# Strips added by transfers, unused matmuls and late loads of modes in an attention and spectral-convolution kernel

## The chip, the cores and the metric

The kernel runs on one core of a Trainium2 chip. The metric is the time of one launch on the device, in microseconds (us). A core has a matrix engine (TensorE, PE in the profile, with PEld for the loading of its stationary operand), VectorE (DVE), ScalarE (ACT), GpSimd (POOL) and SyncE (SP). Each engine works through its own instructions in order and waits on semaphores for what other engines produce. Transfers (DMA) are issued from the queues of SP, ACT and POOL and are carried out by 16 DMA engines. Matmul results land in PSUM, which has eight banks of 512 float32 columns for each of 128 partitions; everything else on the chip is in SBUF. TensorE does not always run at its full clock: the profile lists the clock that was granted to it, as a share of full speed.

## The reference

Four images of 64 channels and 96 x 96 pixels go through two layers with a residual each. The first is self-attention with a sigmoid in place of a softmax, followed by a gate for each channel; the second is a convolution that is done on 16 x 32 modes of a two-dimensional Fourier transform.

```python
def _L0_conv_ref(x, wq, bq, wk, bk, wv, bv, ca_w1, ca_w2):
    ...
    energy = jnp.einsum('bcn,bcm->bnm', Q, K)
    att = jax.nn.sigmoid(energy)
    out = jnp.einsum('bcm,bnm->bcn', V, att).reshape(B, C, H, W)
    out = out + x
    avg = out.mean(axis=(2, 3))
    mx = out.max(axis=(2, 3))
    ...
    scale = jax.nn.sigmoid(mlp(avg) + mlp(mx))
    return out * scale[:, :, None, None]

def _L1_conv_ref(u, W_pos_re, W_pos_im, W_neg_re, W_neg_im):
    ...
    u_hat = jnp.fft.rfft2(u, norm='ortho')
    top = jnp.einsum('bchw,cohw->bohw', u_hat[:, :, :k_h, :k_w], R_pos)
    bot = jnp.einsum('bchw,cohw->bohw', u_hat[:, :, H - k_h:, :k_w], R_neg)
    ...
    return jnp.fft.irfft2(v_hat, s=(H, W), norm='ortho')

x = x + _L0_conv_ref(_gn(x), ...)
x = x + _L1_conv_ref(_gn(x), ...)
```

`_gn` subtracts the mean and divides by the standard deviation of groups of two channels.

## The kernel before

The four images are two pairs; a pair's 2 x 64 channels fill the 128 partitions, and its 9216 pixels are the columns. A pair's pixels are cut into 18 blocks of 512 columns for the attention, and into 12 strips of 768 columns (eight rows of pixels, `STRIP`) for the second layer.

**Opening.** The first pair's nine pieces of 1024 columns come in through the queues of SP and ACT (L100). For each block VectorE takes statistics (`bn_stats`, L516) as it arrives, and beside it TensorE does a matmul whose result nobody reads (`warm`, L551 to L555, 256 columns, into bank 7; loop at L557 to L561, for the first 15 blocks). A 512-column one (L563) comes after the last step of the statistics. Small matmuls (L134, L142) average over groups; then the blocks are normalised (L151), and keys (L418), first queries (L459) and values (L429) are projected, with more `warm` matmuls between them.

**Attention.** For each block of 512 queries and each chunk of 128 keys TensorE does the energies (L474), ScalarE the sigmoid (L485), and TensorE the values times it (L503), which sums up in bank 0 or 7. This runs for both pairs, 36 blocks in all, in an order that the program lays out in lists (`mid`, `end`). While the second pair's attention runs, the second layer of the first pair is done in small steps between it (`Hidden`), its transfers all on SP's queue.

**Between attention and second layer, second pair.** After the last block `after(1)` (L525 to L549) takes mean and maximum over the pixels, does two small matmuls (L539, L544), and a sigmoid on ScalarE gives `gate`. `mv` is the mean after the gate (L762); a small matmul (L134) averages it over groups.

**Strips of the second pair.** Each strip becomes gate times the attention's result plus the image's original values, which were loaded again into the space of `vT` (called `again`, L688). For the strips named in `ADDED` ScalarE multiplies (L773) and a transfer issued by POOL adds (`accum_op`, L774); for the others VectorE does both in one instruction (`combine`, L164). Then VectorE transposes the strip in blocks of 32 (L781), ScalarE squares it for the variance (L782), and TensorE does three matmuls of the transform along the image's rows (L789) into `pa`. There are four strips to one `pa`; when they are done VectorE transposes it (`a`, L799), and two pairs of matmuls (`along_h`, L801) add to `pu`. The transposed strips rotate through four places (`t0` to `t3`). A scheduler that knows durations puts each engine's instructions in order; `tc.issue_after(x)` holds what is in it behind the instruction x.

**Modes and the way back.** With mean and rstd (L145 on POOL, L175) known, `pu` is scaled to `u` (L837 to L844). For eight groups of four mode rows, q = 0 to 7, `mix` (L192) multiplies with the weights (L205), two halves each, copied out of PSUM by VectorE and ScalarE in turn (L118, L120) into `vms[q]`. The weights of 32 rows come by transfers of 512 KB on POOL's queue: 9 during the attention (L680), 6 before the strips, 9 into `vT` once squares no longer need it (L821), and 8 into places of the strips (L733). The modes are turned by a round trip through DRAM: `vms[q]` is stored to `vd` (L217 whole, in turns on SP and POOL, for q up to 6; in four pieces of 64 KB, L221, for q = 7), and `vt` is loaded from it (L235, four loads of 64 KB for each half of the rows): the first half when q = 5 has been stored, on POOL's queue; the second when q = 7 has, on SP's and ACT's. TensorE then transforms back along height (`pz`, L868) and width (`py`, L887), VectorE adds to x1 (L889), and 24 transfers store the result (L892).

`occupy(n, behind, pool)` (L747 to L753) puts n unused matmuls of 512 columns behind a given instruction into a bank of its own: four behind the rstd's matmuls, ten behind the last of `mix`, two behind the last of `pz`.

Of the kernel before, what the change touches and what calls it, by code (L numbers as in the profile page):

```python
# [40 lines left out]
P = 128  # L41
B, C, H, W = 4, 64, 96, 96
# [3 lines left out]
R = C // 16  # L46
KW = 16
KH = 32
NB = 512
NBLK = N // NB  # L50
NCH = N // P
# [7 lines left out]
SIDE = 4  # L59
# [3 lines left out]
SQ = 32  # L63
NSQ = H // SQ
NSTRIP = N // STRIP
ADDED = (3, 6, 9)
GN_EPS = 1e-5


# [13 lines left out]
def tile_kernel(ctx: ExitStack, tc: tile.TileContext, x, cst, late, spec, out):  # L83
    nc = tc.nc
# [8 lines left out]
    cs = const.tile([P, NCONST], F32, tag="cs", name="cs")  # L93
    xs = []
    for p in range(NPAIR):
        xt = xpool.tile([P, N], F32, tag=f"x{p}", name=f"x{p}")
        for s in range(9):
            cols = bass.ts(s, N // 9)
# [7 lines left out]
    vT = xpool.tile([P, NCH, P], F32, tag="vT", name="vT")  # L106

    def named(name, rows=P):
        return cs[:rows, PLACE[name]]
# [43 lines left out]
    class Layer1:  # L153
# [38 lines left out]
        def mix(self, q, half):  # L192

            pv = self.bank(f"pv_{self.p}_{q}_{half}")  # L200
            for k in range(2):
                kw = half * 2 + k
                for g in range(4):
                    at = ((4 * q + g) * KW + SIDE * kw) * 4
                    self.last = nc.tensor.matmul(  # L205
                        pv[bass.ts(g, 32), :].rearrange("q (n k o) -> q n k o", n=SIDE, o=C)[
                            :, :, k, :],
                        self.ut[:, at:at + 32],
                        self.wts[4 * q + g].rearrange("q (n k o) -> q n k o", n=SIDE, o=C)[
                            :, :, kw, :], start=True, stop=True)  # L210
            vm = self.vms[q].rearrange("q (n m) -> q n m", n=SIDE)
            self.move(vm[:, :, bass.ts(half, 2 * C)], pv.rearrange("q (n m) -> q n m", n=SIDE))
            if half == 0:
                return

            if q < KH // 4 - 1 and self.p == 1:
                self.queues[q % 2].dma_start(  # L217
                    self.vd[4 * q:4 * q + 4].rearrange("h s m -> (h s) m"), self.vms[q])
            else:
                for g in range(4):  # L220
                    self.queues[g % 3].dma_start(self.vd[4 * q + g, :4 * SIDE],  # L221
                                                 self.vms[q][32 * g:32 * g + 4 * SIDE, :])

            if q in (5, 7):
                if self.vt is None:
                    self.vt = self.place_of_vt()
                row, M = 32 * KW * C, KW // SIDE * C
                first = KH // 2 * (q == 7)
                for b in range(2):
                    for slot in range(2):  # L230
                        to = 64 * b + 32 * slot + first
                        of = self.vd[first, 2 * slot + b, :]
                        of = bass.AP(tensor=of.tensor, offset=of.offset,
                                     ap=[[row, 16], [4 * KW * C + M, SIDE], [1, M]])
                        self.queues[1 if q == 5 else 2 * slot].dma_start(  # L235
                            self.vt[to:to + 16, :].rearrange("h (n m) -> h n m", n=SIDE), of)

    class Hidden(Layer1):

# [135 lines left out]
    with tc.tile_pool(name="work", bufs=1) as work, \  # L375
# [6 lines left out]
        banks = ps_s.tile([P, 8, NB], F32, tag="banks", name="banks")  # L382
        spare = [0]

        at = attp.tile([P, 14, NB], F32, tag="at", name="at")
# [13 lines left out]
            return u, h  # L399

        projected = [None]
        mark = [None]

        def low_or_high(dst, u, h, is_low):
# [72 lines left out]
        def place(i):  # L477

            t = burst[i]
            return 7 * (t % 2 + 1) - sizes[t] + i - total[t - 1]  # L480
# [16 lines left out]
        def attend(items):  # L497
            for pair, cols in items:
                n, j = divmod(pair, NCH)
                acc = banks[:, 7 - n % 2 * 7, :]  # L500
                for b in range(2):
                    half = slice(b * C, (b + 1) * C)
                    nc.tensor.matmul(acc[half, cols], vT[:, j, half], at[:, place(2 * pair + b), cols],  # L503
                                     start=(j == 0), stop=(j == NCH - 1))
                if j == NCH - 1 and cols.stop == NB:
                    p, m = divmod(n, NBLK)
                    blk = xs[p][:, bass.ts(m, NB)]
                    nc.vector.scalar_tensor_tensor(blk, acc, 1.0, blk, ALU.mult, ALU.add,  # L508
                                                   accum_out=sums[p][:, m:m + 1])
                    mark[0] = nc.vector.tensor_reduce(maxs[p][:, m:m + 1], blk, AX.X, ALU.max)  # L510
# [14 lines left out]
        def after(p):  # L525

            f = small.tile([P, 2], F32, tag="f", name=f"f_{p}")
            hid = small.tile([2 * R, 2], F32, tag="hid", name=f"hid_{p}")
            gate = small.tile([P, 1], F32, tag="gate", name=f"gate_{p}")

            def means():
                tot = small.tile([P, 1], F32, tag="tot", name=f"tot_{p}")
                nc.vector.tensor_reduce(tot, sums[p], AX.X, ALU.add)
                nc.vector.tensor_scalar(f[:, 0:1], tot, 1.0 / N, None, ALU.mult)
                nc.vector.tensor_reduce(f[:, 1:2], maxs[p], AX.X, ALU.max)

            def hidden():
                ph = bank_a(f"ph_{p}")
                nc.tensor.matmul(ph[:2 * R, 0:2], named("w1"), f, start=True, stop=True)  # L539
                nc.vector.tensor_scalar(hid, ph[:2 * R, 0:2], 0.0, None, ALU.max)  # L540

            def gates():
                pg = bank_a(f"pg_{p}")
                nc.tensor.matmul(pg[:, 0:2], named("w2", 2 * R), hid, start=True, stop=True)  # L544
                gsum = small.tile([P, 1], F32, tag="gsum", name=f"gsum_{p}")
                nc.vector.tensor_reduce(gsum, pg[:, 0:2], AX.X, ALU.add)
                nc.scalar.activation(gate, gsum, AF.Sigmoid)

            return gate, [means, hidden, gates], f  # L549
# [7 lines left out]
        each, norm0, _ = stats_of(0)  # L557
        for s, step in enumerate(each):
            last = step()
            if s < NBLK - 3:  # L560
                warm(s, NB // 2)  # L561
        with tc.issue_after(last.ins):
            warm(NBLK - 3)  # L563
# [9 lines left out]
        q = first_queries()  # L573
# [58 lines left out]
        first = begins[NBLK]  # L632
# [64 lines left out]
        for t in range(T):  # L697
# [15 lines left out]
            for step in end[t]:  # L713
                step()
        gate, steps, f = after(1)
        for step in steps:
            step()


    with tc.tile_pool(name="tail", bufs=1, reuse_waits="tile") as tail, \  # L720
# [26 lines left out]
        def occupy(n, behind, pool):  # L747


            pd = pool.tile([P, NB], F32, tag="idle", name=f"idle_{behind.ins.name}")  # L750
            with tc.issue_after(behind.ins):
                for _ in range(n):
                    nc.tensor.matmul(pd, cs[:, :P], cs[:, :NB], start=True, stop=True)  # L753
# [2 lines left out]
        l1 = Layer1(1, gate, lambda name: small_bank.tile([P, NB], F32, tag="m", name=name),  # L756
                    evacuate, (nc.sync, nc.gpsimd, nc.scalar))
        l1.wts = wts
        x1 = xs[1]

        mr, steps, mv = group_stats(None, l1.bank, "l1_1")
# [92 lines left out]
        for q in range(KH // 4):  # L854
            l1.mix(q, 0)
            l1.mix(q, 1)
        occupy(10, l1.last, mix_bank)


        banks.close()  # L860
# [118 lines left out]
```

## Time and profile before

| | |
|---|---|
| median of three runs | 3089.66 us (3088.97 to 3090.65) |
| the profiled execution | 3088.47 us |
| span in it, first to last instruction | 3086.7 us |
| TensorE busy | 3062.3 us (99%) |
| ScalarE busy | 2423.9 us (79%) |
| VectorE busy | 387.6 us (13%) |
| mean granted clock of TensorE | 0.996 |
| last attention matmul ends | about 2998.9 us |
| strips, from the gate to the last `pu` matmul | 3002.0 to 3031.5 us |
| mixing (L205) | 3036.24 to 3050.3 us |
| `pz` starts | 3059.29 us |

A row of a timeline or of the groups gives start or busy time, the engine, the line of the code, the operation, the tile written and the tiles read, and shapes and number. In brackets behind a row stands how long the engine had been idle before it, and what released it. A row of a stretch gives its ends and length, the busy time (and number of instructions) of PE, PEld, DVE, ACT and POOL in it, the granted clock, the mean busy share of the 16 DMA engines, and GB/s. The chain is followed backwards from the last instruction, at each step to what released it. Outside the three regions named in the table (opening, strips, way back) TensorE is occupied by the attention without a gap that matters.

### The profile page before, as it was taken

To read this page: it belongs to the slowest core of one execution; us is meant where nothing else is said; L and a number is where in the kernel's file an instruction comes from. 1 tells how busy PE (TensorE), PEld (TensorE's weight loads), DVE (VectorE), ACT (ScalarE), POOL (GpSimd) and SP (SyncE) were. 2 spreads that over 40 slices of the span, in tenths; PEclk is the share of its full clock that TensorE was granted. 3 is DMA by queue.
4 is the path that set the end of the run, shared out by engine and by line. 5 is a ranking of instruction groups with operands and counts; after the bars stand their busy time and mean duration, and the time that the engine had idled before them with its cause. 6 is when DMAs were issued, how large, how long until landed. Compare 5 with 4: busy or idle time off the path is not lost.

```text
span 3086.7 us, 42551 instructions
## 1 busy us (share of the span) xinstructions
PE 3062.3 (99%) x18910; PEld 1136.5 (37%) x18910; DVE 387.6 (13%) x818; ACT 2423.9 (79%) x1586; POOL 27.1 (1%) x52
## 2 busy tenths in 40 slices
PE   8999999999999999999999999999999999999998
PEld 4333333333333333334433333333333333333336
DVE  5200000000000000002312101010011000000015
ACT  4788888888888888887788887777777888888871
POOL 0000000000000000000000000000000100000001
PEclk9999999999999999999999999999999999999998
DMA  3000000000000000000134120322101300000026
GB/s 144 1 1 1 1 1 1 1 1 1 1 1 1 1 1 1 1 1 1 33 73 96 44 79 21 127 72 39 34 31 42 121 1 1 1 1 1 6 69 239
DMA packets 80488, 99.46 MB, mean 32 GB/s; under 512 B 48208, under 2 KB 58192, under 8 KB 80208
## 3 DMA queue, kind: packets, MB, share of 16 engines
q1 hardware_dynamic: 72032, 71.64, 8.2%
q0 software_dynamic: 5776, 20.45, 1.9%
q10 hardware_dynamic: 2496, 4.65, 0.4%
q8 instruction: 148, 2.42, 0.3%
q14 instruction: 36, 0.29, 0.0%
HBM read 67.49 MB, written 28.05 MB: 31 GB/s over the span
## 4 chain that ended last, share of the span: by engine, by line
PE 98%; DVE 1%; DMA 1%; issue 0%; SPq 0%; ACT 0%; ACTq 0%; DVEq 0%
PE banks L503 75%; PE banks L474 17%; PE banks L429 1%; PE banks L442 1%; PE banks L367 1%; PE banks L418 1%; PE banks L205 1%; PE py L887 0%; PE pv L205 0%; DMA x<-in_x_dram 0%; PE pa L789 0%; PE banks L345 0%; DVE x L164 0%; PE pu L801 0%; PE banks L293 0%; DVE xt L781 0%
## 5 line engine op out<-in xcount | busy, mean ns | idle before, releaser
L485 ACT ACTIVATE at<-banks 128x1536 f32<-128x1536 f32 (+1 forms) x1546 | 2401.4, 1599 | 589.8 <-PE banks L474 536.3
L503 PE MATMUL banks<-at,vT 128*64 128x512 f32 (+1 forms) x11728 | 2394.5, 549 | 0.0
L503 PEld LDWEIGHTS banks<-at,vT 128*64 128x64 f32 x11728 | 780.4, 136 | 1356.2 <-issue 1301.4
L474 PE MATMUL banks<-q,kT 32*128 32x512 f32 x5040 | 550.2, 453 | 0.0
L474 PEld LDWEIGHTS banks<-q,kT 32*128 32x128 f32 x5040 | 223.8, 182 | 455.9 <-issue 303.3
L508 DVE SCALAR_TENSOR_TENSOR x<-banks,x 128x512 f32<-128x512 f32 x36 | 24.9, 691 | 965.2 <-PE banks L503 965.2
L397 DVE TENSOR_SCALAR full_q<-banks,cs 128x256 f32<-128x256 f32 x35 | 16.9, 484 | 957.8 <-PE banks L442 957.8
L429 PE MATMUL banks<-cs,x 128*64 128x128 f32 x576 | 39.8, 279 | 0.7 <-DVE at L461 0.4
L452 DVE CAST q<-q 32x256 fp32r<-32x256 f32 x140 | 39.8, 284 | 3.8
L370 DVE TENSOR_TENSOR x<-banks,x 128x384 f32<-128x384 f32 x24 | 13.4, 557 | 197.0 <-PE banks L367 197.0
L429 PEld LDWEIGHTS banks<-cs,x 128*64 128x64 f32 x576 | 30.9, 136 | 14.6 <-DVE full_k L397 13.5
L406 DVE SCALAR_TENSOR_TENSOR q<-high_q,cs,full_q 64x256 fp32r<-64x256 f32 x70 | 33.6, 480 | 2.4
L397 DVE TENSOR_SCALAR full_k<-banks,cs 128x256 f32<-128x256 f32 x36 | 17.4, 484 | 92.0 <-PE banks L418 92.0
L636 DVE COPY ws<-banks 128x512 f32<-128x512 f32 x16 | 11.1, 691 | 134.6 <-PE banks L205 114.4
L433 DVE TENSOR_TENSOR vT<-banks,cs 128x512 f32<-128x512 f32 x36 | 24.8, 688 | 7.5 <-PE banks L429 7.4
L510 DVE TENSOR_REDUCE maxs<-x 128x1 f32<-128x512 f32 x36 | 24.7, 686 | 1.2
L418 PE MATMUL banks<-x,cs 128*64 128x256 f32 x144 | 23.7, 389 | 0.2 <-DVE full_q L397 0.2
L516 DVE BATCH_NORM_STATS2 stats<-x 128x6 f32<-128x512 f32 x36 | 22.2, 681 | 5.7 <-DMA x<-in_x_dram 5.4
L442 PE MATMUL banks<-x,cs 128*64 128x256 f32 x140 | 22.7, 403 | 0.0
L789 PE MATMUL pa<-xt,lc 128*128 128x256 f32 x72 | 18.9, 419 | 3.5 <-DVE xt L781 3.5
L367 PE MATMUL banks<-cs,ws 128*64 128x384 f32 x96 | 20.8, 512 | 0.0
L554 PE MATMUL banks<-x 128*128 128x256 f32 (+1 forms) x40 | 13.6, 484 | 6.0 <-DMA x<-in_x_dram 6.0
(129 smaller groups left out, 458.0 us busy)
## 6 DMA issues: line engine op xcount, KB each, us to landing
ws<-in_spec_dram SPq DMA_DIRECT2D x20, 512.0 KB
x<-in_x_dram SPq DMA_DIRECT2D x14, 512.0 KB
room<-in_spec_dram SPq DMA_DIRECT2D x12, 512.0 KB
w<-in_spec_dram POOLq DMA_DIRECT2D x10, 512.0 KB, 7.8
old<-in_x_dram SPq DMA_DIRECT2D x12, 384.0 KB
x1d<-x SPq DMA_DIRECT2D x12, 384.0 KB
xd<-old SPq DMA_DIRECT2D x12, 384.0 KB
xT<-xd SPq DMA_DIRECT2D x36, 128.0 KB
```

Of the source, the lines that this page charges most:

```text
L205: self.last = nc.tensor.matmul(pv[bass.ts(g, 32), :].rearrange("q (n k o) -> q n k o", n=SIDE, o=C)[:, :, k, :], self.ut[:, at:at + 32], s ...
L367: nc.tensor.matmul(py[bass.ts(b, C), :4 * W], self.z[:, i, bass.ts(b, C)], named("gw"), start=True, stop=True)
L397: nc.vector.tensor_scalar(u, src, bias, None, ALU.add)
L406: mark[0] = nc.vector.scalar_tensor_tensor(dst, h.bitcast(F32), is_low, u, ALU.mult, ALU.add)
L418: projected[0] = nc.tensor.matmul(pp[cols, :NB // 2], named("wk")[:, cols], src[:, e, :, :], start=True, stop=True)
L429: projected[0] = nc.tensor.matmul(pp[bass.ts(e, P // 2), bass.ts(i, P)], xs[p][:, bass.ts(2 * (4 * s + i) + e, P // 2)], named("wv"), star ...
L442: projected[0] = nc.tensor.matmul(pq[rows, :half], named("wq")[:, rows], xs[p][:, n * NB + e * half:n * NB + (e + 1) * half], start=True, ...
L452: nc.vector.tensor_copy(q[to:to + 32, cols], q[of:of + 32, cols])
L474: nc.tensor.matmul(banks[:, bank_of(t) + i - starts[t], :], kT[r:r + 32, i // 4, :], q[r:r + 32, :], start=True, stop=True)
L485: nc.scalar.activation(at[:, of + lo:of + hi, :], banks[:, bank + lo:bank + hi, :], AF.Sigmoid)
L503: nc.tensor.matmul(acc[half, cols], vT[:, j, half], at[:, place(2 * pair + b), cols], start=(j == 0), stop=(j == NCH - 1))
L508: nc.vector.scalar_tensor_tensor(blk, acc, 1.0, blk, ALU.mult, ALU.add, accum_out=sums[p][:, m:m + 1])
```

## The change

It has four parts.

- Opening: the loop that puts an unused 256-column matmul beside the statistics of a block does so for all 18 blocks.
- Between the values and the gate: an unused matmul of 512 and one of 256 columns, into bank 3, are put behind the last attention matmul, and four of 512 columns (`occupy`) behind the second small matmul of the gate. To name these two places, `attended` and `projected` now remember the instructions.
- Strips: `ADDED`, counted from 0, is 6, 8 and 10 in place of 3, 6 and 9.
- End: the loads of `vt` become a function of their own, `back`. For the first pair they stay where they were. For the second, the first half's loads come behind the last store of q = 7, followed by the second half's. The four last stores go to the queues of SP, ACT, ACT and POOL (pieces 0, 2, 3, 1) in place of SP, POOL, ACT, SP (pieces 0, 1, 2, 3). The number of unused matmuls behind the mixing is nine, not ten.

```diff
-ADDED = (3, 6, 9)
+ADDED = (6, 8, 10)
...
-                for g in range(4):
-                    self.queues[g % 3].dma_start(self.vd[4 * q + g, :4 * SIDE],
-                                                 self.vms[q][32 * g:32 * g + 4 * SIDE, :])
-
-            if q in (5, 7):
-                if self.vt is None:
-                    self.vt = self.place_of_vt()
-                row, M = 32 * KW * C, KW // SIDE * C
-                first = KH // 2 * (q == 7)
-                for b in range(2):
...
+                for g in (0, 2, 3, 1):
+                    stored = self.queues[min(g, 2)].dma_start(
+                        self.vd[4 * q + g, :4 * SIDE], self.vms[q][32 * g:32 * g + 4 * SIDE, :])
+
+
+            if self.p == 0 and q in (5, 7):
+                self.back(q)
+            elif q == 7:
+                with tc.issue_after(stored.ins):
+                    self.back(5)
+                self.back(7)
+
+        def back(self, q):
+            if self.vt is None:
+                self.vt = self.place_of_vt()
+            row, M = 32 * KW * C, KW // SIDE * C
+            first = KH // 2 * (q == 7)
+            for b in range(2):
+                for slot in range(2):
+                    to = 64 * b + 32 * slot + first
+                    of = self.vd[first, 2 * slot + b, :]
+                    of = bass.AP(tensor=of.tensor, offset=of.offset,
+                                 ap=[[row, 16], [4 * KW * C + M, SIDE], [1, M]])
+                    self.queues[1 if q == 5 else 2 * slot].dma_start(
+                        self.vt[to:to + 16, :].rearrange("h (n m) -> h n m", n=SIDE), of)
...
+        attended = [None]
...
-                    nc.tensor.matmul(acc[half, cols], vT[:, j, half], at[:, place(2 * pair + b), cols],
-                                     start=(j == 0), stop=(j == NCH - 1))
+                    attended[0] = nc.tensor.matmul(
+                        acc[half, cols], vT[:, j, half], at[:, place(2 * pair + b), cols],
+                        start=(j == 0), stop=(j == NCH - 1))
...
-                nc.tensor.matmul(pg[:, 0:2], named("w2", 2 * R), hid, start=True, stop=True)
+                projected[0] = nc.tensor.matmul(pg[:, 0:2], named("w2", 2 * R), hid,
+                                                start=True, stop=True)
...
-            if s < NBLK - 3:
+            if s < NBLK:
                 warm(s, NB // 2)
...
         gate, steps, f = after(1)
+        with tc.issue_after(attended[0].ins):
+            for n in (NB, NB // 2):
+                nc.tensor.matmul(banks[:, 3, :n], cs[:, :P], cs[:, :n], start=True, stop=True)
...
         l1.wts = wts
+        occupy(4, projected[0], small_bank)
...
-        occupy(10, l1.last, mix_bank)
+        occupy(9, l1.last, mix_bank)
```

More of the change, by code (lines that the diff above doesn't have):

```diff
@@ L219, in mix @@
             else:
-                for g in range(4):
-                    self.queues[g % 3].dma_start(self.vd[4 * q + g, :4 * SIDE],
-                                                 self.vms[q][32 * g:32 * g + 4 * SIDE, :])
-            if q in (5, 7):
-                if self.vt is None:
-                    self.vt = self.place_of_vt()
-                row, M = 32 * KW * C, KW // SIDE * C
-                first = KH // 2 * (q == 7)
-                for b in range(2):
[L230 to L236, printed above, removed]
+                for g in (0, 2, 3, 1):
[20 more added lines that the diff above has]
+                        self.vt[to:to + 16, :].rearrange("h (n m) -> h n m", n=SIDE), of)
     class Hidden(Layer1):
```

## The prediction

> **What bounds the kernel now.** I read the page first: its parts 1 and 4 say which engine sets the end, and the row of clocks in part 2 says where that engine is slowed.
>
> ```profile
> span 3086.7 us, 42551 instructions
> ...
> PEclk9999999999999999999999999999999999999998
> ...
> PE 98%; DVE 1%; DMA 1%; issue 0%; SPq 0%; ACT 0%; ACTq 0%; DVEq 0%
> ```
>
> TensorE carries 98% of the chain, and the attention (L503, L474) is 92% of it. None of the edits adds or removes an instruction between about 40 us and 2999 us, so some 2960 us stay as they are, and the case is about the first 30 us and the last 90. I therefore asked for the chain in order of time there, for the timeline of TensorE and VectorE, and for busy time and clock in short stretches. The chain of the last 90 us (start, us, what):
>
> ```profile
> 3013.95 2.70 DVE xt L781 x3
> 3016.65 0.04 issue
> 3016.69 1.56 PE pa L789 x6
> 3018.26 1.92 PE pu L801 x8
> 3020.17 5.38 PE pa L789 x24
> ...
> 3029.47 2.01 PE pu L801 x8
> ...
> 3051.36 4.45 DMA vd<-vm
> ...
> 3055.90 3.15 DMA vt<-vd
> 3059.05 0.25 issue
> 3059.29 4.61 PE pz L868 x32
> ```
>
> The reader is to see two hand-overs: VectorE holds the strips up to 3016.65 us and TensorE, never idle again, from there to 3031.48; and at the end two transfers in a row, stores of the modes (vd) and loads of them turned (vt), hold everything for 8 us. The same stretches with the clock that TensorE was granted (the number before the last two):
>
> ```profile
> 15.58:18.99 3.41, 0.80 (x5) 0.71 (x6) 2.36 (x6) 0.00 (x0) 0.00 (x0) 1.00 1.02 407
> 18.99:22.40 3.41, 3.41 (x8) 1.00 (x8) 1.70 (x5) 0.00 (x0) 0.56 (x1) 0.50 1.03 411
> ...
> 2998.82:3002.23 3.41, 0.63 (x6) 0.39 (x4) 2.19 (x11) 0.41 (x2) 0.00 (x0) 1.00 0.44 115
> 3002.23:3005.64 3.41, 1.09 (x3) 1.00 (x4) 3.41 (x6) 3.41 (x6) 2.38 (x3) 0.50 0.31 58
> 3005.64:3009.05 3.41, 3.41 (x9) 2.70 (x8) 3.41 (x5) 2.76 (x6) 1.41 (x3) 0.50 1.04 186
> ```
>
> A stretch in which TensorE did 0.6 to 0.8 us of work is followed by one at half clock, once after the statistics and once after the attention.
>
> **What the Trainium skill says.** "TensorE: Matmul & The Clock Gate", Part 1: The HAM clock gate, says that the clock halves after an idle window of about 3.4 us, comes back after a busy one, and that the windows run free of the kernel. This trace agrees: half clock lasts 18.99 to 22.40 (3.41 us) and 3002.23 to 3009.03 (6.80 us, two windows). So before, the place of the slow stretch differs from run to run. "DMA: Bandwidth & Descriptors", Issuing engines are not separate DMA queues, says that transfers issued by different engines share the same 16 DMA engines and interleave; that bears on the last edit, and the stretch 3051 to 3054.5 (DMA share 1.00, below) agrees.
>
> **The change, part by part.** Times are in the profiled execution, 3088.47 us long with a span of 3086.7; the median of the three runs is 3089.66.
>
> *Opening.* The unused matmuls on x run for all 18 blocks, not 15: three more of 256 columns. Six records took 1.56 us at 13.12, so TensorE works until about 16.24 rather than 14.68, and the statistics matmul comes at 17.49: no delay. The idle time between 14.68 and the 512-column filler at 18.82 (two tiny matmuls aside) is 4.1 us, longer than a window; it becomes 2.6. If the clock then stays full, the filler of 1.91 us takes 0.86 and the first keys no longer wait for it: block 0 is normalised by 20.37, keys take about 0.5 instead of 1.05 (to 21.0), their bias on VectorE 0.48 (to 21.5), the first query matmul 0.87 (to 22.4), and its bias starts at 22.5 instead of 23.63. That is 1.1 us, on the chain. A window placed so that it covers the remaining gap can still halve the clock; if work of under some 30% of a window halves it (23% did, at 15.58), a window must start within about 1.2 us of each 3.41 for that, one run in three, and in before within 2.8, four in five: an estimate. The difference of medians is then about half a step to one step: 0 to 1.1, taken as 0.65.
>
> *Between values and gate.* A filler of 512 and one of 256 columns are put behind the last attention matmul, four of 512 behind the gate's. By the four fillers at 3031.69 (0.86 us each at full clock) the first two take 1.3 us, 2998.9 to 3000.2; the gate's first matmul comes at 3000.74: free. The other four must wait for the sum of the gate, at 3001.75, and take 3.44: until 3005.25. The mean's matmul (L134), queued behind them, ends at 3005.55; its reader on VectorE comes only at 3021. The first strip's matmuls then start at 3005.55 instead of 3005.11, a loss of 0.45, but at full clock: strip 0 ends at 6.9 rather than 7.8. Is that worth anything? In before TensorE waits anyway at strip 3 until 3014.98, behind VectorE. I stepped both queues by the measured durations (combine 0.93, transpose 0.90, transpose of a 1.19, three strip matmuls 1.345, a pu pair 0.95) in the two programs' instruction orders. For before this gives 3031.2 (measured 3031.48); before with the fillers alone 3031.2 again. Alone they are worth 0; cover: VectorE.
>
> *Strips.* Strips 6, 8 and 10 are scaled on ScalarE and added by a transfer, instead of 3, 6 and 9; as many as before, so no work is added. What moves is VectorE's order:
>
> ```profile
> 3007.66 0.97 DVE L781 STREAM_TRANSPOSE xt<-x 128x768 f32<-128x768 f32 x1
> ...
> 3012.13 1.90 DVE L164 SCALAR_TENSOR_TENSOR x<-x,gate,vT 128x768 f32<-128x768 f32 x2
> 3013.95 2.69 DVE L781 STREAM_TRANSPOSE xt<-x 128x768 f32<-128x768 f32 x3
> 3016.57 1.25 DVE L799 STREAM_TRANSPOSE a<-pa 128x1024 f32<-128x1024 f32 x1
> ```
>
> The three transposes at 3013.95 are strips 3, 8 and 6: strip 3 stands behind the combines of 4, 5, 7, 8 and 10, so the first quarter's transpose (a, at 3016.57) and all its matmuls come late. After, strip 3 is combined and transposed with strip 2, by 3009.6, and a_0 follows strip 4 at 3012.3. Stepped in the same way, TensorE ends the strips at 3029.3 instead of 3031.2: 1.9 us. What is late next is TensorE itself, busy from 3012.4 with waits of under 0.1 us. The added strips landed in before 4.0 to 7.5 us after issue, so by about 3012.4; they are wanted at 3014.4, 3016.2 and 3020.8: hidden. Half clock up to 3009 would cost the new order only 0.1, up to 3011 1.1: here the fillers insure. POOL's queue also moves: five weight loads stand behind the rstd step on it rather than three before and two behind. Their issues stay near 3028 to 3031 while the mixing starts 1.9 us earlier. Rows 24 and later are used some 10.3 us into the mixing, at 3044.7, and landed 4.9 to 9.2 us after issue: hidden, about 4 us to spare.
>
> *End.* On the second pair of images the first half of the vt loads (four on POOL) goes behind the last stores, the last stores are SP one, ACT two, POOL one rather than SP two, ACT one, POOL one, and nine fillers follow instead of ten.
>
> ```profile
> 3048.39 0.54 POOL L235 DMA_DIRECT2D vt<-vd  x1 [3.57 <-PE pv L205]
> 3048.92 0.54 POOL L217 DMA_DIRECT2D vd<-vm  x1
> 3049.45 1.55 POOL L235 DMA_DIRECT2D vt<-vd  x3
> 3051.24 0.51 POOL L221 DMA_DIRECT2D vd<-vm  x1 [0.23 <-ACT vm L120]
> ```
>
> The store of vm 5 waited behind a load for 3048.39, though ScalarE had finished its half at 3047.5. And the DMA engines stood still just then:
>
> ```profile
> 3048.00:3049.50 1.50, 1.50 (x36) 1.09 (x32) 0.48 (x1) 0.58 (x1) 1.11 (x3) 1.00 0.05 14
> ...
> 3051.00:3054.50 3.50, 3.50 (x9) 1.52 (x8) 0.00 (x0) 0.00 (x0) 0.51 (x2) 1.00 1.00 307
> ...
> 3055.00:3057.00 2.00, 2.00 (x6) 0.95 (x5) 0.00 (x0) 0.00 (x0) 0.00 (x0) 1.00 0.02 3
> ```
>
> After, that store goes out 1.4 us earlier into the idle stretch, and 256 KB of loads leave the queue ahead of the last stores; these should be down near 3054 instead of 3055.8. The POOL loads are issued from 3051.75 to 3053.9 and flow while the stores' completion is awaited; with the 4.7 us median of such loads the last lands at 3058.6 at worst, with the 2.3 minimum at 3056.2. The last four loads (3.15 us) then end near 3057. Nine fillers of 0.86 end at 3058.2 where ten ended at 3059.05, so TensorE's fillers, not the loads, become what pz waits for: 0.9 us saved, bounds 0 and 1.1. If the loads are late, pz starts with them and the saving shrinks.
>
> Sum: 0.65 + 0 + 1.9 + 0.9 = 3.45 us. From the median, 3089.66 − 3.45 = 3086.2. From the profiled execution, which had its half clock, 3088.47 − (1.1 + 1.9 + 0.9) = 3084.6; three runs of before spread over 1.7 us, so I keep both in the range.
>
> **Rivals.**
> (a) Only the strips pay: the opening keeps its half clock by the phase of the windows and pz waits for POOL's late loads. 3089.66 − 1.9 = 3087.8. For it: the loads' spread of 2.3 to 5.1 us; against: idle DMA engines.
> (b) Slower: POOL's loads behind the last stores. Place: the four vt loads. Transfers issued on POOL took up to 9.2 us when the engines were full; the last, issued at 3053.9, would land at 3063.1, 4.0 us after 3059.05. Against 0.65 + 1.9 gained: 3091.1. It decides once the last load takes more than about 7.7 us. Against it: only 512 KB is in flight then.
> (c) Nothing moves: VectorE's total work for the strips is unchanged, and TensorE's too, so the order gives nothing: 3089.6. Against it: TensorE idles 3.5 us before strip matmuls.
> (d) More than the sum: every part at its upper bound and the wandering windows gone: 3083 or less.
>
> **How the numbers follow.** Forecast 0.60, (a) 0.24, (b) 0.08, (c) 0.04, (d) 0.04. What a measurement of this kernel can tell from no change is about 0.2%, 6.2 us. Forecast, (a), (c) and nearly all of (b) lie inside. Faster by more: 0.05; slower by more, (b) with a second mishap: 0.03; within: 0.92. The range 3084.2 to 3088.8 holds the forecast from its upper bounds to (a) with the spread of the runs.
>
> **What would show it.** Right: no half clock near 3002 to 3009; pu's last matmul near 3029.3 less what the opening saved; strip 3's transpose directly behind strip 2's; the DMA engines busy near 3048.5; pz right behind the ninth filler. Wrong: a half-clock stretch after 3005 that delays strips, TensorE waiting for an added strip, or pz waiting for a POOL load.

## The result and the profile after

The changed kernel takes 3085.78 us, the median of 22 runs (3084.67 to 3086.72), against 3089.84 us for the kernel before in the same comparison (22 runs, 3088.21 to 3090.80): a ratio of 0.9987, 95% interval 0.9981 to 0.9993. The difference of 4.06 us is smaller than the 6.2 us that the prediction gave as what can be told from no change; the interval excludes no change all the same.

The profiled execution of the changed kernel took 3084.82 us. The first lines of its page (span, granted clock in 40 slices) and the line of the chain's shares:

```profile
span 3082.9 us, 42582 instructions
...
PEclk9999999999999999999999999999999999999998
...
PE 98%; DVE 1%; DMA 0%; issue 0%; SPq 0%; POOL 0%; ACT 0%; DVEq 0%
```

TensorE holds the chain as it did; DMA alone has left it (1% to 0%). At this scale nothing else is to be seen, so the two executions are cut into stages at events which both have. Each row is worked out from the starts and ends in the two traces:

| stage | before, us | after, us | difference |
|---|---|---|---|
| start to the last attention matmul's end | 2998.87 | 2998.16 | −0.71 |
| strips: from there to the last `pu` matmul's end | 32.56 | 30.71 | −1.85 |
| scaling to `u`, until mixing starts | 4.81 | 5.06 | +0.25 |
| mixing | 14.02 | 14.02 | 0 |
| end of mixing to the first `pz` matmul | 9.03 | 7.85 | −1.18 |
| `pz` to the last addition | 22.30 | 22.31 | +0.01 |
| last addition to the end | 5.11 | 4.83 | −0.28 |
| span | 3086.70 | 3082.95 | −3.75 |

The matmuls' ends in the trace overlap a little with the next one's start, so a chain, which counts from end to end, puts `pz` 0.07 us later than this table where it follows a filler (7.92 for 7.85 below).

The stages after the attention repeat well: mixing is 14.02 us in all eleven kernels that were profiled for this case, `pz` to the last addition 22.28 to 22.33, and the strips 32.56 or 32.57 in the five that have the old `ADDED`. So these stages resolve a tenth of a microsecond where the time of a run, which spreads over more than 2 us, doesn't. The way from the mixing to `pz` does so only where the unused matmuls end it: the four kernels that have before's stores, loads and ten unused matmuls take 8.71, 8.71, 8.94 and 9.03 us, and before's own profile is the longest of them.

The chain of waits of the changed kernel over the last 90 us (start, us, what), at the places shown of before:

```profile
3010.52 0.98 DVE xt L796
...
3011.54 1.56 PE pa L804 x6
3013.11 1.92 PE pu L816 x8
3015.03 7.97 PE pa L804 x36
...
3026.92 2.01 PE pu L816 x8
...
3033.94 14.02 PE pv L205 x256
3047.96 7.92 PE idle_I-15028_15043 L767 x18
3055.88 4.57 PE pz L883 x32
```

Two things differ. TensorE takes over from VectorE at 3011.54 instead of 3016.69 us, behind a single transpose (strip 4's) where three stood; and `pz` is released by the unused matmuls (L767), where before the chain went through a store and a load. What VectorE does up to that point (timeline of VectorE):

```profile
3006.94 1.83 DVE L796 STREAM_TRANSPOSE xt<-x 128x768 f32<-128x768 f32 x2
3008.70 1.91 DVE L164 SCALAR_TENSOR_TENSOR x<-x,gate,vT 128x768 f32<-128x768 f32 x2
3010.52 0.97 DVE L796 STREAM_TRANSPOSE xt<-x 128x768 f32<-128x768 f32 x1
3011.41 1.21 DVE L814 STREAM_TRANSPOSE a<-pa 128x1024 f32<-128x1024 f32 x1
```

The pair at 3006.94 is strips 2 and 3, then come the combines of 4 and 5, strip 4's transpose, and at 3011.41, 5.16 us earlier than before, the first quarter's transpose `a`. The clock and busy time in stretches as long as a window at the two places which had a half-clock stretch before (where the windows' edges lie can't be seen at full clock; ends and length, busy time and number on PE, PEld, DVE, ACT and POOL, clock, DMA share, GB/s):

```profile
15.69:19.10 3.41, 1.36 (x8) 0.87 (x7) 2.36 (x6) 0.00 (x0) 0.00 (x0) 1.00 1.02 408
19.10:22.51 3.41, 2.90 (x10) 1.08 (x10) 2.36 (x6) 0.00 (x0) 0.56 (x1) 1.00 1.03 410
2998.00:3001.41 3.41, 2.54 (x11) 1.36 (x10) 2.08 (x10) 0.30 (x2) 0.00 (x0) 1.00 0.41 115
3001.41:3004.82 3.41, 3.41 (x11) 1.51 (x9) 3.41 (x6) 3.41 (x6) 2.27 (x3) 1.00 0.27 50
...
3045.70:3047.20 1.50, 1.50 (x36) 1.09 (x32) 0.47 (x1) 0.58 (x1) 0.31 (x1) 1.00 0.53 210
```

The clock is full throughout the first four. The last one lies as far ahead of the end of the mixing (2.26 to 0.76 us) as 3048.00 to 3049.50 did before; there the DMA engines are busy for 53% of the time instead of 5%. POOL's timeline says why:

```profile
3045.48 0.53 POOL L217 DMA_DIRECT2D vd<-vm  x1 [2.97 <-ACT vm L120]
3048.93 0.50 POOL L221 DMA_DIRECT2D vd<-vm  x1 [2.92 <-ACT vm L120]
3049.67 2.05 POOL L243 DMA_DIRECT2D vt<-vd  x4 [0.24 <-issue]
```

The store of `vm` 5 goes out as soon as ScalarE has written it (its wait ends with ScalarE), and the four loads follow POOL's last store.

### The profile page after: what moved, and what is told of

Its sections match the earlier page's. It is cut to its first block, busy times and chain, and to the rows that moved or that the text cites. A ratio compares the mean times of both kernels' runs of the same rounds, so it can differ in the third digit from the quotient of the medians.

```text
span 3082.9 us, 42582 instructions
## 1 busy us (share of the span) xinstructions
PE 3064.7 (99%) x18926; PEld 1138.0 (37%) x18926; DVE 387.5 (13%) x818; ACT 2424.0 (79%) x1586; POOL 27.1 (1%) x52
## 4 chain that ended last, share of the span: by engine, by line
PE 98%; DVE 1%; DMA 0%; issue 0%; SPq 0%; POOL 0%; ACT 0%; DVEq 0%
PE banks L512 76%; PE banks L483 17%; PE banks L438 1%; PE banks L451 1%; PE banks L375 1%; PE banks L205 1%; PE banks L427 1%; PE py L902 0%; PE pv L205 0%; DMA x<-in_x_dram 0%; PE pa L804 0%; PE banks L353 0%; PE idle_I-15028_15043 L767 0%; PE pu L816 0%; PE banks L301 0%; DVE x L164 0%
```

## The experiments

The question is how much each part carries, and whether the parts add up. Five kernels do one part of the change, or half of one, alone; four undo or shift one in the changed kernel. The times are compared with runs of the kernel before made beside them on the same chip; the stages come from one profiled execution each.

### The opening alone

```diff
-            if s < NBLK - 3:
+            if s < NBLK:
```

> The kernel before with the opening's loop over all 18 blocks, nothing else. Theory 1 (the three extra matmuls keep the clock full through the first projections): the first query bias starts some 0.7 us earlier after the end of the statistics, no half-clock stretch between 17 and 23 us in its profile, and the strips keep their half-clock stretch after 3002; the time falls by about 0.65 us (0 to 1.1). Rival (the opening waits for the statistics and the rstd on POOL anyway, the clock is indifferent): the query bias at the same distance from the end of the statistics, time unchanged.

Measured: 3088.70 us (13 runs), before 3089.78 (41 runs), ratio 0.9996, interval 0.9988 to 1.0005. The medians differ by 1.1 us, which the interval alone doesn't establish. In the profile no half clock is left at the opening: from the start of the statistics' last step to the first query's bias it takes 6.05 us instead of 6.83. Everything behind the attention is as before (strips 32.56, `pz` 8.71 behind the mixing), with its half clock.

What the recorded estimate had left out is seen in the kernels without this edit. In the profile of one of them (only the ninth filler removed, below), the same stretch takes 8.02 us, because not one window but two are at half clock. The stretches at its opening:

```profile
14.24:17.65 3.41, 0.71 (x4) 0.28 (x2) 3.38 (x6) 0.00 (x0) 0.00 (x0) 1.00 1.04 412
17.65:21.06 3.41, 2.62 (x6) 1.43 (x6) 1.30 (x7) 0.00 (x0) 0.56 (x1) 0.50 1.02 407
21.06:24.47 3.41, 3.41 (x9) 1.51 (x9) 1.70 (x4) 0.00 (x0) 0.00 (x0) 0.50 1.03 411
```

The window after the idle one still has idle time in it (2.62 us of work in 3.41), and the next is at half clock too; behind that one, which is full, the clock comes back. The mean clock of a run tells whether two windows were lost: profiles of before's structure with two slow windows at the opening and two at the strips show 0.995, with one and two 0.996. Of the 115 runs of before, on three chips, 77 show 0.995, with medians of 3089.95 to 3090.26 us by chip, and 38 show 0.996, with 3088.59 to 3089.11. By the profiles one window costs 0.8 to 1.4 us, by its place (6.83 to 7.45 against 6.04 or 6.05), and two 1.6 to 2.0 (7.65 to 8.02), each up to the first query's bias; before mostly had two.

The edit makes the half clock rarer and doesn't rule it out. 1 of this kernel's 13 runs shows 0.995. Of the six profiled kernels with the edit, three have no half clock at the opening (this one, the changed kernel, the one with eight unused matmuls), one has one window and two have two; all five without it have one or two. Read in the same way (where the clock stays full at the strips, two windows show as 0.996 and none as 0.997), 14 of the 103 runs with the edit had two windows, 1 of them among the changed kernel's 22.

### The matmuls between values and gate alone

```diff
+        with tc.issue_after(attended[0].ins):
+            for n in (NB, NB // 2):
+                nc.tensor.matmul(banks[:, 3, :n], cs[:, :P], cs[:, :n], start=True, stop=True)
...
+        occupy(4, projected[0], small_bank)
```

> The kernel before with the two and the four unused matmuls between the values and the gate, nothing else. Theory 1 (in the old order of strips VectorE is what TensorE waits for, so a full clock buys nothing): no half clock from 3002 to 3009, yet from the last attention matmul to the last pu matmul it stays 32.6 us within 0.2, and the time unchanged within 0.3 us. Rival (the half clock is what made the strips late): this stretch gets shorter by 1 to 2 us, and so does the time.

Measured: 3089.75 us, ratio 0.9999 (0.9991 to 1.0007). The half clock between attention and strips is gone and the stage of the strips is 32.56 us, as before. The timeline of TensorE shows what it waits for at full clock:

```profile
3013.38 1.56 PE L796 MATMUL pa<-xt,lc 128*128 128x256 f32 x6 [0.72 <-DVE xt L788]
3016.09 1.56 PE L796 MATMUL pa<-xt,lc 128*128 128x256 f32 x6 [1.16 <-DVE xt L788]
3017.81 1.56 PE L796 MATMUL pa<-xt,lc 128*128 128x256 f32 x6 [0.16 <-DVE xt L788]
```

TensorE waits 0.72, 1.16 and 0.16 us for VectorE's transposes of the strips (releaser `DVE xt`). The last two waits stand in before too (1.15 and 0.15); the first, and one of 0.36 us ahead of it, are new: there the time that full clock saves is waited away again. With the old strips the clock costs nothing, because VectorE is late. (The matmuls move VectorE's order a little here too, one transpose ahead of one combine, but `a` starts 17.71 us behind the attention as it did before, 17.70.)

### The strips alone

```diff
-ADDED = (3, 6, 9)
+ADDED = (6, 8, 10)
```

> The kernel before with strips 6, 8 and 10 added by transfers, nothing else. Theory 1: from the last attention matmul to the last pu matmul 30.8 us instead of 32.6 where the half clock ends by 3009, up to 1.1 more where it lasts until 3011; time lower by 1.2 to 1.9 us. Rival (order and clock are needed together): less than half of that.

Measured: 3089.03 us, ratio 0.9996 (0.9988 to 1.0005). The stage takes 31.71 us: a gain of 0.85, less than half of the 1.85 in the changed kernel. Two things in the profile differ from the changed kernel's. First the order on VectorE, although the program text of the strips is the same; the last row is TensorE's:

```profile
3009.91 1.90 DVE L164 SCALAR_TENSOR_TENSOR x<-x,gate,vT 128x768 f32<-128x768 f32 x2
3011.73 1.83 DVE L781 STREAM_TRANSPOSE xt<-x 128x768 f32<-128x768 f32 x2
3013.49 0.97 DVE L164 SCALAR_TENSOR_TENSOR x<-x,gate,vT 128x768 f32<-128x768 f32 x1
3014.38 1.24 DVE L799 STREAM_TRANSPOSE a<-pa 128x1024 f32<-128x1024 f32 x1
...
3015.67 1.99 PE L801 MATMUL pu<-a,lc 64*128 64x512 f32 x8 [0.84 <-DVE a L799]
```

Behind the combines of 4 and 5 come two transposes (4 and 5) and the combine of 7 before `a`; in the changed kernel one transpose. The scheduler knows durations, and with the unused matmuls on TensorE it comes to another order. Second, the half clock, from 3002.97 to 3009.79; but in this order TensorE waits 0.84 us for `a`, so the clock isn't what makes it late here.

### The changed kernel without the matmuls between values and gate

The diff is the one of the gate, taken back in the changed kernel.

> The changed kernel without the unused matmuls between the values and the gate. Theory 1 (in the new order of strips they are only an insurance against the wandering half clock): half clock again after 3001, the last pu matmul later by 0 to 1.1 us; time higher by 0.1 to 1.0 us with more spread. Rival (the new order brings the gain with or without them): unchanged within 0.1 us. Second rival (they carry the gain): higher by 1.5 us or more.

Measured: 3086.38 us (13 runs), before 3089.82 (41), ratio 0.9991 (0.9983 to 0.9999). The strips take 31.71 us again, in the same order as with the strips alone, so what the matmuls are worth in the changed kernel is 1.00 us of the stage; alone they were worth 0. The time lies 0.6 us above the changed kernel's, in the range of the first theory; its reason, an insurance against the half clock, is only part of it, as the next run shows. This kernel's profile also has half clock at the opening in spite of the edit there, for two windows; the first of them and the one ahead of it:

```profile
16.47:19.88 3.41, 1.57 (x6) 0.82 (x6) 1.75 (x6) 0.00 (x0) 0.53 (x1) 1.00 1.02 407
19.88:23.29 3.41, 2.93 (x8) 1.42 (x8) 2.27 (x5) 0.00 (x0) 0.04 (x1) 0.50 1.03 411
```

### The changed kernel's order, written out, without those matmuls

The run before leaves two readings: the matmuls act through the scheduler's order, or through the clock. Here the order is forced and the clock left to drop; the six matmuls are taken out as above.

```diff
-            if s not in ADDED:
+            if s in (7, 9, 11):
+                with tc.issue_after(turned[0].ins):
+                    l1.combine(s, again[:, cols])
+            elif s not in ADDED:
...
-            nc.vector.transpose(xt, x1[:, cols])
+            with tc.issue_after(turned[0].ins) if s == 5 else nullcontext():
+                nc.vector.transpose(xt, x1[:, cols])
...
-            nc.vector.transpose(a, pa.rearrange("q (h c) -> q c h", c=SQ))
+            turned.append(nc.vector.transpose(a, pa.rearrange("q (h c) -> q c h", c=SQ)))
```

> The changed kernel without the six unused matmuls between values and gate, but with strip 5's transpose and the combines of strips 7, 9 and 11 held behind the transpose of the first quarter (a), so that VectorE and TensorE do the strips in the changed kernel's own order. The stage is measured from the last attention matmul to the last pu matmul: 30.71 us in the changed kernel, 31.71 without the fillers. Theory A (the fillers act through the order that the scheduler chooses when it knows of them): the stage is 30.7 to 31.2, although the clock is still at half for a while behind the attention; the time is within 0.6 us of the changed kernel's 3085.8. Theory B (the fillers act through the clock that they keep up): the stage stays near 31.7, with a half-clock stretch in the region of the strips, and the time near 3086.4 to 3086.8. If the profile shows no half clock there at all, B isn't tested and only the order's share is seen.

Measured: 3086.37 us (13 runs), before 3089.77 (33), ratio 0.9988 (0.9980 to 0.9996). The stage takes 31.22 us, just above the range of the first theory and well below 31.7: it is both. The timeline of VectorE:

```profile
3010.14 1.90 DVE L164 SCALAR_TENSOR_TENSOR x<-x,gate,vT 128x768 f32<-128x768 f32 x2
3011.97 0.97 DVE L796 STREAM_TRANSPOSE xt<-x 128x768 f32<-128x768 f32 x1
...
3013.68 1.25 DVE L814 STREAM_TRANSPOSE a<-pa 128x1024 f32<-128x1024 f32 x1 [0.51 <-PE pa L804]
```

It is the changed kernel's order (but for two steps of under 0.2 us that stand elsewhere), but VectorE stands idle for 0.51 us ahead of `a`, which is released by TensorE's `pa`; in the changed kernel no idle time stands there. TensorE has no wait left in these five strips and is late because its clock was at half up to 3010.65, 11.04 us behind the attention (stretches of 3 us; the third number from the end is the clock):

```profile
3004.00:3007.00 3.00, 1.16 (x3) 0.98 (x4) 3.00 (x4) 3.00 (x6) 2.68 (x3) 0.50 0.56 102
3007.00:3010.00 3.00, 3.00 (x9) 2.37 (x8) 3.00 (x4) 2.14 (x6) 1.29 (x3) 0.50 1.06 188
3010.00:3013.00 3.00, 3.00 (x14) 2.58 (x13) 2.98 (x5) 1.85 (x4) 0.37 (x1) 0.89 1.02 171
```

So the 1.00 us is 0.49 of order (31.71 to 31.22) and 0.51 of clock (31.22 to 30.71). The 0.51 is there when TensorE goes on to the `pu` matmuls: 15.38 us behind the attention, in the changed kernel 14.88. The clock's share holds for this place of the windows, which run free: in the kernel without the matmuls the half clock ended 9.52 us behind the attention. And it needs the better order: in the worse one TensorE waited 0.84 and 0.93 us for `a` at half clock, so that a full clock had nothing to shorten there. No kernel with the worse order at full clock was run.

### Nine unused matmuls instead of ten, alone

```diff
-        occupy(10, l1.last, mix_bank)
+        occupy(9, l1.last, mix_bank)
```

> The kernel before with nine unused matmuls behind the mixing instead of ten, nothing else. Theory 1 (the loads land at 3059.05, when the tenth ends, so pz waits for them): from the end of the mixing to pz stays 9.0 us within 0.2, and pz is released by a vt load; time unchanged within 0.3 us. Rival (the number of unused matmuls alone set the end): 8.1 us, and 0.86 us off the time.

Measured: 3089.78 us, ratio 1.0000 (0.9992 to 1.0008). `pz` starts 8.86 us behind the mixing instead of 9.03. The chain ahead of it:

```profile
3052.92 4.19 DMA vd<-vm
...
3057.21 3.23 DMA vt<-vd
3060.43 0.25 issue
3060.68 3.40 PE pz L868 x24
```

Store and load hold `pz`, 0.94 us behind the ninth filler's end; a filler less changes nothing that can be told.

### The late loads alone, with ten

The diff is the change's for `back` and the four last stores; ten unused matmuls stay.

> The kernel before with the loads of modes behind the last stores and the new queues for these, but still ten unused matmuls. Theory 1 (the loads land some 1 to 2 us earlier, but the tenth unused matmul still ends where it ended): from the end of the mixing to pz 8.8 to 9.0 us, pz right behind the tenth; time lower by 0 to 0.3 us. Rival (loads on POOL behind the last stores come late): over 9.0 us, pz released by a vt load.

Measured: 3089.59 us (13 runs), before 3089.82, ratio 0.9999 (0.9990 to 1.0007). `pz` starts 8.71 us behind the mixing instead of 9.03 (8.78 in the chain), and the chain shows what it waits for:

```profile
3036.24 14.02 PE pv L205 x256
3050.26 8.78 PE idle_I-15018_15033 L761 x20
3059.04 4.57 PE pz L876 x32
```

Now the tenth filler holds it. Against before's 9.03 us the halves of this part bring 0.17 and 0.32 us alone and 1.18 together: each hides the other. But `pz` stands right behind the tenth filler, at 8.71 us, in two kernels with the old loads as well (the opening alone, the strips alone). Before's loads landed late enough to cost 0.32 us in its own profile and not in these, so the loads alone bring 0 to 0.32, and both together 0.86 (one filler) to 1.18.

### Eight in the changed kernel

```diff
-        occupy(9, l1.last, mix_bank)
+        occupy(8, l1.last, mix_bank)
```

> The changed kernel with eight unused matmuls behind the mixing instead of nine. Theory 1 (the fillers bound the end; the last load's bytes are there at 3055.05 in the changed kernel's profile, pz starts at 3055.88): pz then waits for the loads, and from the end of the mixing to pz it is 7.4 to 7.7 us instead of 7.92; time lower by 0.2 to 0.5 us. Rival (the loads already bound it): 7.9 us, no gain.

Measured: 3085.87 us (21 runs), ratio 0.9988 (0.9981 to 0.9994), the same as the changed kernel within what can be told; the 0.2 to 0.5 us of the first theory did not come. `pz` starts 7.76 us behind the mixing, against 7.85 with nine, and the chain goes through a transfer again:

```profile
3049.11 2.74 DMA vd<-vm
...
3051.95 3.57 DMA vt<-vd
3055.51 0.25 issue
3055.76 4.61 PE pz L883 x32
```

`pz` waits for a load, as the first theory had it, but for one that is ready within 0.1 us of the ninth filler's end: nine fits, and with the transfers of this profile no more is to be had from the fillers.

### One transpose earlier

```diff
-            if s not in ADDED:
-                l1.combine(s, again[:, cols])
+            with tc.issue_after(turned[0].ins) if s >= 5 else nullcontext():
+                if s not in ADDED:
+                    l1.combine(s, again[:, cols])
...
-            nc.vector.transpose(xt, x1[:, cols])
+            step = nc.vector.transpose(xt, x1[:, cols])
+            if s == 4:
+                turned.append(step)
```

> The changed kernel with the combines and transposes of strip 5 and later held behind strip 4's transpose, so that VectorE does c4, x4, c5, a where the changed kernel does c4, c5, x4, a. Theory A (VectorE sets the first quarter of the strips, TensorE the rest, and is hardly late any more): a gain of 0.1 to 0.2 us in the stage, 30.5 to 30.6 instead of 30.71, nothing that the time can tell from the changed kernel's 3085.8. Theory B (VectorE's order still costs as much as the half microsecond of one combine and transpose before a): 30.2 or below. If the stage gets longer, above 30.9, VectorE is late for a strip after the quarter, and the changed kernel's own order is the better.

Measured: 3085.69 us (21 runs), ratio 0.9988 (0.9981 to 0.9994); the strips take 30.55 us, 0.16 less than in the changed kernel, as the first theory expected. In time it can't be told from the changed kernel. None of the nine beats the changed kernel by an amount that these runs resolve.

## Why the prediction was right, and where its steps were not

The total was right: the sum of 3.45 us stands against 4.06 in the medians and 3.75 in the two profiles. That two changes which no step had, +0.25 and −0.28, cancel is luck. The steps, in the prediction's order:

- **Opening, 0.65: mis-sized.** "That is 1.1 us, on the chain" lies among the 0.8 to 1.4 us that one half-clock window cost, though the window of the profile it was read from is worth 0.78 (6.83 to 6.05). But before had two in 77 of 115 runs, which cost 1.6 to 2.0, and the sum has only one; and "if work of under some 30% of a window halves it" sets the limit too low: 1.57 us of 3.41 (46%) halved it in the kernel without the gate's matmuls. The chances that it gave, four in five before and one in three after, stand against five of five and three of six profiles. The part came to 1.1 in the medians of the edit alone, with an interval that doesn't exclude none. The estimate should have come from more than one execution: it read the number of slow windows off a single profile.
- **Gate alone, 0: right**, and for the reason given: the timeline names VectorE as what TensorE then waits for.
- **Strips, 1.9: right in the sum (1.85), wrong in what pays it.** The failed step is that the stepping put the changed program's order down to `ADDED` and the matmuls at the gate to insurance ("here the fillers insure"). `ADDED` alone gives 0.85. The order that was stepped is the one the scheduler makes with the unused matmuls in the program; without them it makes a worse one. Of the 1.85, 0.85 are the strips, 0.49 the order that the matmuls bring with them, and 0.51 the clock. The stepping itself was sound: it gave 1.9 for this order as a whole, which needs no right account of who makes the order, and half clock up to 3009 or 3011 us was to cost 0.1 or 1.1; in the frame of before it lasted to 3009.9 in the experiment (2998.87 + 11.04) and cost 0.51.
- **Weights behind the rstd step, hidden: right for the transfers, wrong by 0.25 for what lies beside.** Mixing starts with its weights and runs 14.02 us unbroken. But the stage ahead of it is longer by 0.25 us, which no step had. It is longer in the three kernels whose POOL timeline has six weight loads in a row behind that step (the prediction named five; before has two pairs there, where it read two loads): 5.06 to 5.11 us in the changed kernel, with eight fillers, and with one transpose earlier; 4.81 in the three with the new strips but without the gate's matmuls, which have five. The last section shows the rows.
- **End, 0.9: right in mechanism, 1.18 in size.** "TensorE's fillers, not the loads, become what pz waits for" is what the chain shows, to the ninth. The ninth filler's end less the tenth's, 0.86, is exact: between the kernels with the late loads it is 8.71 to 7.85. The other 0.32 is what before's loads, which landed behind the tenth filler, cost in its own profile, 9.03 against 8.71; the sum took `pz` as if it stood at the tenth filler's end, and in two of the four kernels with this end it does. Rival (b), the loads on POOL coming late, had no part: POOL issued them 1.71 us behind the mixing (3049.67), 0.2 later than assumed (3051.75, 1.49 behind it), but they landed 2.5 to 3.0 us after issue, the last 5.80 behind the mixing, where (b) had up to 9.2.
- **Not in the sum:** −0.28 us between the last addition and the end. It goes with the opening's edit (4.77 to 4.84 us in most kernels with it, 4.48 in one, 5.11 to 5.43 in those without). Why is open; no run was made for it.

Rival (a), "only the strips pay", falls: with strips alone the time is 3089.03, and the way to `pz` did shorten. Rival (c), that the order gives nothing, falls with the stage of the strips, and (d), 3083 or less, with the time.

## What to carry to other kernels

Where a scheduler that knows durations writes the order, an instruction that does nothing can move others: compare each engine's order with and without it before its worth is put down to the clock or to anything else, and force the order in an experiment to tell them apart. Two measures that are worth little or nothing alone can be worth a microsecond together when each hides the other, as a filler and a transfer did here; name for each what would be late next, and test the pair. Where times of runs can't resolve a part, cut the profiled spans at events that all versions share, but take what depends on the free-running clock windows from the clocks of many runs, and what waits for a transfer from more than one profile.

## What the runs showed of the hardware that was not expected

A window with nearly half its time at work can still halve TensorE's clock: 1.57 of 3.41 us in the run without the gate's matmuls. The Trainium skill, "TensorE: Matmul & The Clock Gate", Part 1: The HAM clock gate, speaks of an idle window and names no share. And a window at half clock with 2.93 of 3.41 us at work, in the same run, did not bring it back: the half clock there lasts for two windows, to 26.71 us. No limit of busy time fits all profiles: with the strips alone a window with 1.64 us of work (12.89 to 16.30) was followed by full clock, and in the kernel with the order written out one with 1.76 (17.16 to 20.58) by half.

The longest half-clock stretch is one that the change doesn't touch. In all eleven profiles the clock halves once more on the way back, 9.9 to 12.6 us after `pz` starts, and stays so to the end, although TensorE is shown busy without a gap on both sides of the drop. Two stretches of before, ahead of the drop and behind it:

```profile
3068.70:3069.70 1.00, 1.00 (x18) 1.00 (x18) 0.60 (x2) 0.00 (x0) 0.00 (x0) 1.00 0.00 0
3072.70:3073.70 1.00, 1.00 (x18) 1.00 (x18) 0.60 (x2) 0.00 (x0) 0.00 (x0) 0.50 0.76 294
```

Here, unlike what that page tells, no idle window goes ahead of the half clock, and busy ones don't end it; why is open. The stage doesn't get longer by it: TensorE's records show 18 to 21 matmuls in a microsecond at either clock, and `pz` to the last addition takes 22.28 to 22.33 us wherever the drop falls.

The scaling of `pu` to `u` is slower in the changed kernel. VectorE's rows of before and after:

```profile
3033.12 0.66 DVE L842 TENSOR_SCALAR u<-t,rs 64x512 f32<-64x512 f32 x1
3033.79 1.16 DVE L840 TENSOR_SCALAR u<-t,rs 64x512 f32<-64x512 f32 x2
```

```profile
3030.56 0.77 DVE L857 TENSOR_SCALAR u<-t,rs 64x512 f32<-64x512 f32 x1
3031.35 1.30 DVE L855 TENSOR_SCALAR u<-t,rs 64x512 f32<-64x512 f32 x2
```

The same instructions take 0.11 and 0.14 us more, together the 0.25 us by which the stage is longer. POOL was issuing weight loads until 3030.90 us, so the first overlaps with it, and the others don't. The Trainium skill, "SBUF — State Buffer", SBUF: two separate sides, says that VectorE and GpSimd share a pair of ports under an exclusive lock, for some kinds of VectorE instruction; whether these are of the kind, no run here shows, and it could account for the first row only. ScalarE's two activations beside them take longer too, 2.31 us instead of 2.13. What slows these and the second row is not settled.
